# Pacing of a background chain: shorter pause in the inverse transform, Gram sums in one row, more table buffers

## The chip, the cores and the metric

The kernel runs on one core of a Trainium2 chip. The metric is the device time of one launch in microseconds, the median of several runs. Before the change it is 6687.31 us, the median of 3 runs from 6674.74 to 6688.99. The engines are TensorE (PE, matmuls), VectorE (DVE), ScalarE (ACT), GpSimd (POOL) and SyncE (SP), each with its own instruction queue that is worked in order. Lines such as L1301 are lines of the kernel before.

## The reference

The input x has 16 images of 32 channels of 128 x 128. Four layers follow one another, each adding its result to its input after a group normalisation `_gn`:

```python
x = x + _L0_conv_ref(_gn(x), ...)  # a recurrence over skewed columns, 128 steps
x = x + _L1_conv_ref(_gn(x), ...)  # 3x3 sums of |patch - weight|, 32 outputs, quantised
x = x + _L2_conv_ref(_gn(x), ...)  # Hartley transform, mix of 32 x 32 modes, transform back
x = x + _L3_conv_ref(_gn(x), ...)  # five edge operators, normed, conv1..conv7 with pooling and upsampling
```

Layer 3 needs, for each image, the mean and the standard deviation of the five edge pictures over all channels and pixels. The kernel gets these from Gram sums: products of neighbouring rows of the picture with themselves, multiplied with fixed tables and summed.

## The kernel before

**Three parts.** Layer 0 runs first (to about 670 us). Then layer 1 runs for the 16 images in turn, the main part, to 5587 us. Layers 2 and 3 run for four groups of four images each: groups 0 to 2 in the background of the main part, one after the other, each once its images are ready; group 3 at the end, together with what is left of group 2. This end is called the drain here.

**The main part** (class `Differences`). For each half image 72 difference tiles are made, one by one on DVE (L760, `d_dve`, 2.36 us) or on ACT (L757, `d_act`, 7.15 us). PE sums each of them into four PSUM banks (L647). Three buffers hold DVE's tiles and two hold ACT's. PE fills gaps with matmuls on zeros (L677, `keep_busy`).

**The order is planned while the program is written out.** Background work (class `After`) is a generator. It yields a positive number for PE work of so many microseconds, a negative one for a pause, or `SUMMED` for "until PE has finished". After each difference tile the main loop calls `Weave.advance`, which takes steps of the generator as long as planned time allows; a pause holds the background back until the planned time of DVE has passed it, so it is in effect rounded up to whole difference tiles. Then `keep_order` fixes the order on every engine. Planned times only set the order; on the chip each engine takes its next instruction as soon as its semaphores allow. `later(us, step)` puts off a step, mostly a DMA on SP, in the same way.

**The drain** (function `drain`) has two such generators, the rest of group 2 on four PSUM banks and all of group 3 on four others. The one whose planned time is less goes next, and pauses are stretched by 1.5. When one has ended, the other runs alone with all eight banks. Group 3 has a copy of the object with buffer counts of its own (`"t_r": 8, "gm": 5, "e_v": 6` among them), so the counts that the diff changes are those of groups 0 to 2.

**A group's chain** is: `forward` (transform, L1103 to L1231), `back` (back products L1278; then 16 iterations of column products L1323 and the take-outs), `statistics` (Gram matmuls L1428, then 20 table sums L1492), scaling of the folded weights (L1559, L1561), `conv1` (L1747, eight chunks of 25 taps), the small convolutions (L1597) and upsamplings (L905), and `last` (L1876).

**The take-out** (`take_out`, L1296) of iteration n adds two PSUM tiles to the residual `xr[n]` (L1301) and takes statistics of it (L1303). Some planned microseconds later the result is stored to DRAM (L1307) and, later again, the residual n + 4 is loaded into the same buffer (`reload`, L1257); both DMAs are on SP. There are four such buffers (`t_r`) for groups 0 to 2. The next iteration's products are issued right behind the take-out, into the PSUM tiles that the take-out before last has freed.

**The table sums** multiply each of four Gram tiles (one an image) with each of five tables `gm`. With three table buffers the fourth and fifth tables are loaded by POOL (L1500) when the first and second have been used. The folded weights `v` come in ten halves through a ring of `e_v` buffers, also loaded by POOL.

Of the kernel before, what the change touches and what calls it, by code (L numbers as in the profile page):

```python
# [350 lines left out]
class Weave:  # L351
# [10 lines left out]
    def __init__(self, work):  # L362
        self.work, self.pending = work, None
        self.pe = self.dve = self.act = self.now = self.base = 0.0
        self.until = self.ready = 0.0
        self.draining = self.alone = False
        self.stretch = 1.0
        self.finished, self.count, self.put_off, self.for_act, self.ends = -1, 0, [], [], {}
# [590 lines left out]
class After:  # L959


    def __init__(self, nc, tc, side, sm, ps, cst, bias, a, d, stat, out):
        self.nc, self.tc, self.side, self.ps, self.cst, self.bias = nc, tc, side, ps, cst, bias
        self.a, self.d, self.stat, self.out = a, d, stat, out
        self.spare, self.banks = None, 0
        self.sm, self.scales = sm, {}
        self.buffers = {"t_x": 4, "xm": 3, "xw": 2, "t_w": 3, "t_r": 4, "frames": 2, "gm": 3, "e_v": 3, "l_x": 2}
        store = [d["up"][i] for i in range(3)]
        self.up5 = Composed(nc, sm, a, "deconv1", "conv5", bias[:, 7:8], bias[:, 4:5], store[0])
        self.up6 = Composed(nc, sm, a, "deconv2", "conv6", bias[:, 8:9], bias[:, 5:6], store[1])  # L970
        self.up7 = Composed(nc, sm, a, "deconv3", "conv7", bias[:, 9:10], bias[:, 6:7], store[2])
# [269 lines left out]
    def back(self, g, load):  # L1241
# [6 lines left out]
        with self.pool("t_z") as zp_, self.pool("t_r", ahead) as rp:  # L1248
# [47 lines left out]
            def take_out(n, pf):  # L1296
                while ready.get(n):
                    weave.done(ready[n])
                for r in range(2):
                    v = xr[n][:, r]  # L1300
                    nc.vector.scalar_tensor_tensor(v, pf[r], 2.0**-15, v, ALU.mult, ALU.add)  # L1301
                for r in range(2):
                    nc.vector.bn_stats(stat[:, 2 * n + r, :], xr[n][:, r])  # L1303
                weave.dve += 2.8

                def store():
                    nc.sync.dma_start(rows(n)(x3), xr[n])  # L1307
                    ready[n + ahead] = weave.later(6.0, lambda: reload(n + ahead)) if n + ahead < 16 else None

                ready[n + ahead] = weave.later(4.0, store)  # L1310
# [6 lines left out]
            for n in range(16):  # L1317
                s, half = n // 2, n % 2
                pf = [self.acc() for _ in range(2)]
                for i in range(4):  # L1320
                    for r in range(2):
                        part = slice(64 * half + 32 * r, 64 * half + 32 * r + 32)
                        nc.tensor.matmul(  # L1323
                            pf[r][:, W * i : W * i + W],
                            o1[part, 4 * s + i].rearrange("p b o -> p (b o)"),
                            cst["cas_t"][part, :],
                            start=True,
                            stop=True,
                        )
                yield 0.8  # L1330
                if previous:
                    yield -3.2
                    take_out(*previous)
                previous = n, pf
            yield SUMMED
# [65 lines left out]
    def statistics(self, g, pool, frames, sides, out, tables):  # L1401
# [12 lines left out]
        gm = [pool.tile([128, GRAM], F32, name="gm", bufs=tables_ahead) for _ in range(tables_ahead)]  # L1414
# [74 lines left out]
        for k in range(5):  # L1489
            for blk in range(4):  # L1490
                w = pool.tile([128, GRAM], F32, name="es_w", bufs=1)
                nc.vector.tensor_tensor_reduce(  # L1492
                    w, gram[blk][:, :GRAM], gm[k], 1.0, 0.0, ALU.mult, ALU.add, accum_out=red[:, blk, k : k + 1]
                )
                weave.dve += 0.7
                if blk % 2:
                    yield -0.4
            if len(gm) < 5:
                gm.append(pool.tile([128, GRAM], F32, name="gm", bufs=tables_ahead))
                nc.gpsimd.dma_start(gm[-1], self.a["gram"][:, len(gm) - 1])  # L1500
# [554 lines left out]
```

## Time and profile before

The profiled execution took 6656.74 us, with a span of 6655.0 us from its first to its last instruction; the median of the timed runs is 6687.31 us.

| stretch | us | what runs |
|---|---|---|
| layer 0 | 0 to about 670 | recurrence |
| main part alone | 683 to 1838 | difference tiles only |
| group 0 | 1838 to 3383 | background beside difference tiles |
| group 1 | 3406 to 4946 | the same |
| group 2, first part | 4963 to 5587 | up to the scaled weights, before conv1 |
| drain | 5590 to 6655 | rest of group 2 and group 3; group 3 alone from about 6317 |

| in the span | PE | DVE | ACT | POOL |
|---|---|---|---|---|
| busy us | 5351.9 | 5541.6 | 5455.3 | 66.4 |
| share | 80% | 83% | 82% | 1% |

A profile line "A <- B: total, times, longest" is the time for which A's engine stood idle before A, and what ended the wait. In a timeline each row has start, duration, engine, line and operation, with the idle time before it in brackets. A matmul of float32 is two records in the trace, so 32 records are 16 matmuls of the program.

### The profile page before, as it was taken

Reading aid. Unit: us, or ns where it says so; the run is one execution under the profiler, and the core shown is the slowest. Engines: PE = TensorE matmul, PEld = TensorE weight load, DVE = VectorE, ACT = ScalarE, POOL = GpSimd, SP = SyncE. Lnnn points to the kernel's source line nnn. Section 1 sums busy time; section 2 is a strip of 40 time slices with the busy share of each in tenths; the row PEclk is TensorE's granted clock in tenths of the full one; section 3 lists DMA queues with packets and bytes.
Section 4 is the critical chain, followed back from the end, with each engine's and each line's share of the span. In section 5 each row is a group of like instructions: output and inputs, shape, how many; then the busy total and the mean of one; then the engine's idle time right before and its main releaser. Section 6 shows DMA issues by size and latency. Waiting matters only on the chain.

```text
span 6655.0 us, 270517 instructions
## 1 busy us (share of the span) xinstructions
PE 5351.9 (80%) x126760; PEld 2793.3 (42%) x126760; DVE 5541.6 (83%) x6848; ACT 5455.3 (82%) x3201; POOL 66.4 (1%) x67
## 2 busy tenths in 40 slices
PE   3698677787777879998877778999787787986896
PEld 3675333333343433333333443333333443444584
DVE  7898899999999889999999999999999996243222
ACT  3898899999999989999999999999999996111112
POOL 0000000000000000000000000000000000000000
PEclk9999899999989989998999899999989898997897
DMA  7553322211343632211553652231355354345314
GB/s 318 209 190 121 80 58 63 54 40 47 76 135 109 185 106 64 66 43 48 115 144 92 176 157 67 66 78 35 79 137 148 88 168 127 133 155 161 100 32 108
DMA packets 380773, 728.15 MB, mean 109 GB/s; under 512 B 73284, under 2 KB 225348, under 8 KB 368772
## 3 DMA queue, kind: packets, MB, share of 16 engines
q1 hardware_dynamic: 372180, 676.41, 35.4%
q0 software_dynamic: 7040, 33.80, 1.5%
q8 instruction: 992, 16.25, 1.0%
q14 instruction: 129, 1.06, 0.1%
q10 hardware_dynamic: 432, 0.64, 0.0%
HBM read 510.69 MB, written 200.00 MB: 107 GB/s over the span
## 4 chain that ended last, share of the span: by engine, by line
issue 33%; PE 29%; DVE 21%; ACT 13%; DMA 4%; SPq 1%; POOL 0%; DVEq 0%; ACTq 0%; POOLq 0%
DVE d_dve L760 12%; PE acc L1747 11%; ACT d_act L757 8%; PE acc L647 7%; PE pg L223 3%; PE acc L905 3%; ACT gt L237 2%; PE acc L1597 1%; DVE stat L124 1%; DVE y L1685 1%; ACT junk L198 1%; PE acc L1428 1%; DMA v<-fold_d 1%; DMA xm_d<-xm 1%; ACT th L247 1%
## 5 line engine op out<-in xcount | busy, mean ns | idle before, releaser
L757 ACT ACTIVATE d_act<-q,neg 128x8192 f16<-128x8192 f16 (+1 forms) x628 | 4443.9, 7150 | 117.1 <-PE acc L647 95.1
L760 DVE TENSOR_SCALAR d_dve<-q,qw 128x8192 f16<-128x8192 f16 (+1 forms) x1676 | 3865.2, 2362 | 165.1 <-PE acc L647 146.1
L647 PE MATMUL acc<-d_dve,sel 128*32 128x512 f16 x26816 | 1874.2, 403 | 491.2 <-DVE d_dve L760 392.6
L647 PEld LDWEIGHTS <-sel 128*32 128x32 f16 x36864 | 1010.6, 100 | 2118.9 <-issue 1461.4
L1747 PE MATMUL acc<-xp,wf 32*32 32x512 f32 x25600 | 1000.9, 610 | 26.0 <-issue 17.5
L647 PE MATMUL acc<-d_act,sel 128*32 128x512 f16 x10048 | 734.1, 414 | 292.4 <-ACT d_act L757 285.3
L1688 ACT ACTIVATE y<-pooled,b 32x128 f32<-32x128 f32 x464 | 185.5, 400 | 513.1 <-DVE pooled L1674 506.8
L1747 PEld LDWEIGHTS acc<-xp,wf 32*32 32x32 f32 x25600 | 422.7, 104 | 373.1 <-issue 292.5
L677 PE MATMUL acc<-q,zero 128*32 128x512 f16 x6268 | 449.3, 399 | 0.0
L905 PE MATMUL acc<-y,u_conv 32*32 32x256 f32 (+1 forms) x9728 | 339.0, 453 | 88.5 <-issue 66.8
L223 PE MATMUL pg<-h,wb 64*64 64x20 f32 (+15 forms) x8192 | 341.4, 305 | 58.8 <-DVE h L251 33.7
L237 ACT ACTIVATE gt<-pg,bias 128x20 f32<-128x20 f32 (+15 forms) x1024 | 332.3, 384 | 40.1 <-PE pg L223 38.1
L223 PEld LDWEIGHTS pg<-h,wb 64*64 64x64 f32 x8192 | 251.5, 151 | 134.2 <-DVE h L251 81.1
L1428 PE MATMUL acc<-xp 32*64 32x204 f32 (+3 forms) x8576 | 241.1, 343 | 42.0 <-issue 40.2
L677 PEld LDWEIGHTS <-zero 128*32 128x32 f16 x6268 | 189.1, 101 | 172.8 <-issue 36.4
L1876 DVE SCALAR_TENSOR_TENSOR xr<-acc,l_one,xr 128x512 f32<-128x512 f32 x128 | 87.1, 743 | 199.0 <-PE acc L905 131.3
L905 PEld LDWEIGHTS acc<-y,u_conv 32*32 32x32 f32 x9728 | 155.6, 109 | 207.2 <-issue 158.1
L1846 ACT ACTIVATE xr<-xr,l_ms 128x1024 f32<-128x1024 f32 x64 | 68.7, 1145 | 209.7 <-DVE xr L1876 199.6
L1428 PEld LDWEIGHTS acc<-xp 32*64 32x64 f32 (+1 forms) x8576 | 170.2, 134 | 123.2 <-issue 115.4
L1782 DVE TENSOR_TENSOR acc<-acc,cut 128x4 f32<-128x4 f32 x256 | 35.3, 165 | 219.3 <-PE acc L1747 217.0
L223 PE MATMUL pg<-xn,wb 64*64 64x2 f32 (+63 forms) x4096 | 184.0, 290 | 25.9 <-issue 17.0
L1597 PE MATMUL acc<-y,w_conv 32*32 32x512 f32 (+2 forms) x4608 | 161.4, 506 | 46.9 <-DMA w_conv<-in_conv_dram 21.3
(218 smaller groups left out, 3653.4 us busy)
## 6 DMA issues: line engine op xcount, KB each, us to landing
q<-q_d SPq DMA_DIRECT2D x128, 536.2 KB, 10.1
xp<-xn_d SPq DMA_DIRECT2D x64, 660.0 KB, 5.0
xp<-x_d SPq DMA_DIRECT2D x56, 640.0 KB, 5.5
xr<-xn_d SPq DMA_DIRECT2D x64, 528.0 KB, 11.7
x_in<-in_x_dram SPq DMA_DIRECT2D x16, 2048.0 KB, 14.7
xn<-in_xs_dram SPq DMA_DIRECT2D x64, 512.0 KB, 7.0
res<-in_x_dram SPq DMA_DIRECT2D x64, 512.0 KB, 8.8
x_d<-res SPq DMA_DIRECT2D x64, 512.0 KB, 4.9
```

What stands on the lines that cost most here:

```text
L223: nc.tensor.matmul(bank[c][q][64 * pair : 64 * pair + 64, :, :width], wb[half, 4 * kind + KIND[q]].rearrange("p b o -> p (b o)"), v[half], ...
L237: nc.scalar.activation(gt[:, q, :, :n], bank[c][q][:, :, :n], AF.Tanh if q == G else AF.Sigmoid, bias=bias[:, KIND[q] : KIND[q] + 1],)
L647: self.nc.tensor.matmul(acc[k][32 * j : 32 * j + 32, :], self.sel16[:, i // 9, :], d[:, row : row + 4, c : c + W], start=first, stop=last,)
L677: self.nc.tensor.matmul(acc[k][32 * j : 32 * j + 32, :], self.zero, q[:, :4, :W], start=False, stop=False)
L757: nc.scalar.activation(dst, src, AF.Relu, bias=self.neg[:, i : i + 1])
L760: nc.vector.tensor_scalar(dst, src, self.qw[:, i : i + 1], 0.0, ALU.subtract, ALU.max)
L905: nc.tensor.matmul(acc[blk][32 * j : 32 * j + 32, o : o + rows * n], t[part, 4 * par + tap, :], src[part, top : top + rows, left : left + ...
L1428: nc.tensor.matmul(gram[blk][j : j + width, at : at + n], xp[part, l, 2 + j : 2 + j + width], xp[part, rows, j : j + width + 4], start=sta ...
L1597: nc.tensor.matmul(acc[blk][32 * j : 32 * j + 32, : rows * n], wc[name][part, tap, :], src[part, at : at + rows, kw : kw + n], start=tap == 0,
L1688: nc.scalar.activation(d, s, AF.Identity, bias=bj)
L1747: nc.tensor.matmul(acc[blk][32 * j : 32 * j + 32, :], tap_of("all", tap)[rows], xp[rows, 4 * j + kh : 4 * j + kh + 4, kw : kw + W], start= ...
L1876: nc.vector.scalar_tensor_tensor(v, acc[blk].rearrange("p (b r w) -> p r w b", b=2, w=64), one[:, blk : blk + 1], v, ALU.add, ALU.mult,)
```

## The change

Three edits. In `After.__init__` the table buffers `gm` go from three to five and the buffers of folded weights `e_v` from three to four. In `back` the pause ahead of each take-out goes from 3.2 to 1.4 planned microseconds. In `statistics` the pause of 0.4 after every second table sum is gone. With five table buffers all five tables are loaded at the start of `statistics`, and the load at L1500 is not reached. The last two edits act in the drain too.

```diff
@@ After.__init__
-        self.buffers = {"t_x": 4, "xm": 3, "xw": 2, "t_w": 3, "t_r": 4, "frames": 2, "gm": 3, "e_v": 3, "l_x": 2}
+        self.buffers = {"t_x": 4, "xm": 3, "xw": 2, "t_w": 3, "t_r": 4, "frames": 2, "gm": 5, "e_v": 4, "l_x": 2}
@@ After.back
                 yield 0.8
                 if previous:
-                    yield -3.2
+                    yield -1.4
                     take_out(*previous)
                 previous = n, pf
@@ After.statistics
                 weave.dve += 0.7
-                if blk % 2:
-                    yield -0.4
             if len(gm) < 5:
```

## The prediction

> **What bounds the kernel now.** I read the page's slices first, then the busy time by stretch, then the waits, then single instructions.
>
> ```profile
> PE   3698677787777879998877778999787787986896
> DVE  7898899999999889999999999999999996243222
> ACT  3898899999999989999999999999999996111112
> ```
>
> There are two regimes. Up to slice 34 VectorE (DVE) and ScalarE (ACT) are full, producing the difference tiles of layer 1; then they go nearly idle and TensorE (PE) carries the end. The last difference tile ends at 5587 us. The busy times (length, PE, PE weight loads, DVE, ACT, POOL, PE clock, DMA share, GB/s):
>
> ```profile
> 683.00:1838.00 1155.00, 898.11 (x15882) 432.19 (x15885) 1134.72 (x878) 1128.46 (x176) 0.00 (x0) 0.94 0.23 57
> 2384.00:2440.00 56.00, 28.17 (x325) 11.39 (x321) 52.80 (x96) 56.00 (x9) 9.54 (x9) 0.73 0.32 103
> 4038.00:4591.00 553.00, 526.98 (x11716) 199.58 (x11716) 519.86 (x331) 540.16 (x190) 0.00 (x0) 0.98 0.22 58
> 5232.00:5347.00 115.00, 87.66 (x1272) 48.11 (x1268) 115.00 (x106) 113.50 (x18) 0.00 (x0) 0.87 0.52 153
> 5860.00:5955.00 95.00, 89.95 (x2166) 51.01 (x2145) 50.15 (x97) 16.08 (x41) 0.00 (x0) 0.93 0.59 184
> 5955.00:6130.00 175.00, 119.11 (x3824) 75.47 (x3812) 57.11 (x199) 38.70 (x66) 5.80 (x11) 0.82 0.60 180
> ```
>
> These are: layer 1 alone; Gram sums and table products; conv1 inside the main part; the take-outs of group 2; the take-outs of group 3 in the drain; group 3's Gram matmuls. The first has 599 tiles in 1155 us, 1.93 us a tile. The background never rests: group 1 begins (3406) when group 0 ends (3383), group 2 (4963) when group 1 ends (4946). So a microsecond saved in any group's chain of steps moves everything after it forward, and more of group 2 is done before the drain.
>
> The pause decides the pace in the drain. DVE around three take-outs of group 3:
>
> ```profile
> 5879.09 1.29 DVE L1301 SCALAR_TENSOR_TENSOR xr<-acc,xr 128x512 f32<-128x512 f32 x2 [4.09 <-PE acc L1323]
> 5880.30 1.28 DVE L1303 BATCH_NORM_STATS2 stat<-xr 128x6 f32<-128x512 f32 x2
> 5885.66 1.29 DVE L1301 SCALAR_TENSOR_TENSOR xr<-acc,xr 128x512 f32<-128x512 f32 x2 [4.09 <-PE acc L1323]
> ```
>
> One iteration is 6.57 us, of which DVE works 2.57 and waits 4.09 for products that stand on PE behind five taps of the other group's conv1. In the main part an iteration of the steady stretch is 6.94 us: two difference tiles (4.67) and 2.6 of take-out. The risk is SyncE's queue, here in group 2:
>
> ```profile
> SPq L1307 <- DVE xr L1301: 118.2, 10, 87.0
> SPq L1257 <- DMA x_d<-xr: 53.5, 11, 13.9
> ```
>
> A residual's reload waits on SP until the store of its buffer has landed, once 13.9 us, while q loads were under way.
>
> **What the Trainium skill says.** "Perfetto Trace Analysis", section Optimization Strategy: where the most-contended engine changes between regimes, interleaving the regimes can help. The trace agrees: in the first stretch PE is busy 898 of 1155 us, so PE work moved there has room. "DMA: Bandwidth & Descriptors", section Anatomy of one DMA: a semaphore wait is made by the issuing sequencer before dispatch; the SP waits above are that. Same page, section Issuing engines are not separate DMA queues: loads issued by POOL share the same 16 engines; no run here separates the two. "TensorE: Matmul & The Clock Gate", section What's actually happening: PE falls to half clock after an idle window of about 3.4 us. The trace agrees in direction: clock 0.73 in the table stretch above.
>
> **The change part by part.** I compared the instruction orders of the two builds; they say where each step stands, not how long it takes.
>
> *Pause -3.2 to -1.4.* Difference tiles issued between first and last take-out of a group: 41, 41, 43 before; 25, 23, 26 after. Nothing is removed; 16 to 18 tiles per group move behind the take-outs.
>
> *Gram sums without pauses.* Only 3, 3, 3 tiles stand between the 20 sums before, 0, 1, 1 after: the sums take about 16 us now, and 20 x (0.594 + 0.082) = 13.5 us of DVE is their floor. At most 3 tiles per group. ACT hides the block with its two buffers (2 x 7.15 us); without that cover 13.5 us of ACT would idle per group.
>
> *Five table buffers.* Six loads of 210 KB move from behind the sums (L1500) to the start of the stage, on POOL, whose 67 busy us are 1% of the span. Their landing (3.6 us median) is hidden by some 130 us of Gram matmuls; without cover it would cost 6 x 3.6 = 22 us. DVE's idle before the sums names only the Gram matmuls as releaser, so I take 0.
>
> *Four fold buffers.* DVE waited for these loads 8.1 us in the whole main part (8 times, longest 2.1). Worth 0 to 8; I take 0.
>
> Sum of the lead: where group 2's table scaling ends, the after-build is 81 tiles earlier. At the last difference tile it has 848 of conv1's 3200 matmuls behind it, where before it had none.
>
> *Main part.* DVE gains 8 poolings (0.688), 16 cut additions (0.165) and 4 copies (estimate 0.2), 8.9 us; its tiles change by +21 x 2.384 - 19 x 2.350 = +5.4: in all +14.3. ACT gains 16 evictions (0.400), 6.4, and its tiles change by +19 x 7.118 - 21 x 7.226 = -16.5: -10.1. Weighted by what each makes (one tile in 2.36 or 7.15 us, shares 0.75 and 0.25): **+8 us**. Cross-check: conv1 inside the main part runs 543 us with 269 tiles, 2.02 a tile, so 74 tiles more of it cost 74 x 0.09 = 7. PE takes the matmuls instead of 592 filler matmuls (L677).
>
> *Drain.* A conv1 tap is 16 matmuls in 1.16 us (32 records in 1.17 us in the timeline), 0.0725 each. Gone: 848 x 0.0725 = 61.5, and about 3.5 of edge matmuls: 65 us. By stage, from matmul counts of the two orders: up to group 3's first back product conv1 has 1936 before, 1952 after, no difference. In the take-outs the other group gives 800 matmuls before, 288 after; DVE becomes the limit there: 16 x 2.57 = 41, plus two rounds of conv2 evictions (8 x about 1.8 = 14), 55 us for 89 (5863 to 5952): -34. From there to group 3's conv1 400 small-conv matmuls less stand against 384 upsampling ones more: 0. After it 384 fewer upsampling matmuls (339 us for 4864, 0.07 each): -27. Together -61. Against it I set 14 us, estimates: 8 for the stores, because 16 stores and 8 reloads of 0.5 MB in 55 us are 229 GB/s where 184 took 0.59 of the DMA engines; and 6 for the unbroken block of sums, behind which the other group's evictions wait on DVE, up to 13.5. **-47 us**.
>
> Sum: 6656.7 - 47 + 8 = 6618 for the profiled execution, -39 us or -0.6%. The profiled execution was 30.6 below the median of the timed runs, so I put the same difference on the median: 6687 - 39 = **6648**.
>
> *What is late next.* The moved tiles lose nothing, but the four residual buffers now turn in four short iterations: 2.6 us of take-out plus some 1.1 tiles, 5.2 us. In the usual new order reload n+4 stands on SP behind store n+1. It lands at about 5.2 + 1 + 4.2 (the median landing) = 10.4 us after take-out n ends; take-out n+4 starts at 4 x 5.2 - 2.6 = 18.2. Slack 7.8 us. Behind that reload SP holds later stores and the q loads for both engines. Where q loads fall into the stage (groups 0 and 2), a store's landing of 14 us instead of 5 uses the slack up: 0 to 12 us in all, inside the range.
>
> **Rivals.** *A, nothing left (6683).* The drain is held by latencies, not PE work: its Gram stretch has PE busy 119 of 175 us, and the upsampling that moves into it waits on evictions. Then only a part of the take-out gain stays, say 12 of 34 after the stores' backlog, against +8: -4. For it: those gaps. Against: the other drain stretches have PE at 90% or more up to 5955.
>
> *B, slower (6729).* The reloads come late in every iteration of the main part. Place: L1301 waiting for the reload of L1257. Price: 36 reloads x 0.75 = 27 us for each microsecond of lateness. It decides once the trip passes 18.2 by 39 / 27 = 1.4 us; at 3 us late, +81 - 39 = +42. For it: the 13.9 us wait and DMA shares of 0.52 to 0.60. Against: reload landings of 3.4 to 4.7 us in that stage, and no DVE wait for a residual before.
>
> *C, all of it (6625).* No backlog, no hold-up by the sums: -61 or a little more, main part nearly free because ACT ends earlier: -62.
>
> *D, the sums and buffers do nothing*, only the pause acts. This is half in the forecast already: 3 tiles, 6 us a group at most.
>
> **How the numbers follow.** Forecast 0.60 (own range 6630 to 6673), A 0.13, B 0.11, C 0.16. A measurement of this kernel can tell about 0.2%, 13.4 us: faster means below 6674. Forecast and C are faster, 0.76; A is within, 0.13; B slower, 0.11. The range 6618 to 6688 leaves out B and part of C.
>
> **What would show it.** Right: take-outs of a main group in 80 to 90 us (103 to 115 now); L1747 records before the last difference tile; that tile at about 5595; group 3's take-outs in about 55 us with no 4 us waits; span near 6618. Wrong: DVE waits at L1301 for a DMA; difference tiles waiting for PE by much more than 146 us; the end of the main part beyond 5610; a longer gap between group 3's take-outs and its Gram matmuls (now 53 us).

## Result and the profile after

The changed kernel takes 6647.09 us (median of 4 runs, 6630.3 to 6654.34) against 6686.53 before (4 runs, 6674.74 to 6688.99): ratio 0.9952, 95% interval 0.9937 to 0.9968. Measured a second time, it took 6640.0 against 6666.88, ratio 0.9960 (0.9948 to 0.9972). So it is faster by 0.4 to 0.5%, 27 to 39 us. Profile against profile it gained 26.4 us, 6656.74 to 6630.3.

The slices of the page after show the same two regimes:

```profile
PE   3698677787777879997887879998877879887896
DVE  7898899999999989998999999999999998242322
ACT  3898899999999999998999989999999998102112
```

The last difference tile ends at 5604 us (5587 before); from there to the end it is 1025 us (1068 before). The main part cost some 15 us, the drain gave 43. Busy times after, with the prediction's columns: take-outs of group 2; conv1 of group 2 inside the main part, which was not there before; take-outs of group 3; group 3's Gram matmuls; the whole drain.

```profile
5126.00:5203.00 77.00, 57.42 (x732) 31.94 (x725) 74.19 (x85) 77.00 (x12) 0.00 (x0) 0.84 0.73 227
5459.00:5604.00 145.00, 136.95 (x3204) 55.65 (x3196) 140.36 (x88) 144.65 (x38) 0.00 (x0) 1.00 0.12 36
5887.00:5964.00 77.00, 60.05 (x1051) 38.88 (x1048) 58.09 (x135) 0.00 (x0) 0.00 (x0) 0.70 0.69 214
5993.00:6136.00 143.00, 100.19 (x3345) 61.26 (x3318) 25.36 (x68) 36.98 (x60) 0.00 (x0) 0.87 0.72 194
5604.00:6628.00 1024.00, 825.12 (x25757) 532.16 (x25746) 312.16 (x866) 177.51 (x339) 7.97 (x15) 0.86 0.43 120
```

The drain of the kernel before, for comparison:

```profile
5587.00:6655.00 1068.00, 874.92 (x27636) 561.26 (x27635) 318.01 (x886) 187.23 (x364) 7.94 (x15) 0.89 0.41 118
```

PE is busy 50 us less in the drain and idle 6 us more (193 to 199), which makes the 43 us less there. In the main part, DVE in the take-outs of group 1 after the change (timeline):

```profile
3653.53 1.29 DVE L1301 SCALAR_TENSOR_TENSOR xr<-acc,xr 128x512 f32<-128x512 f32 x2
3654.73 1.28 DVE L1303 BATCH_NORM_STATS2 stat<-xr 128x6 f32<-128x512 f32 x2
3655.92 2.34 DVE L760 TENSOR_SCALAR d_dve<-q,qw 128x8192 f16<-128x8192 f16 x1
3658.18 1.29 DVE L1301 SCALAR_TENSOR_TENSOR xr<-acc,xr 128x512 f32<-128x512 f32 x2
```

One tile stands for each take-out where there were two, 4.65 us an iteration where it was 6.94, and no idle time in brackets. PE in group 3's take-outs, first before the change, then after it (`...` stands for rows left out):

```profile
5877.90 1.16 PE L1323 MATMUL acc<-cw,o 32*128 32x128 f32 x16
5878.99 5.55 PE L1747 MATMUL acc<-xp,wf 32*32 32x512 f32 x160
```

```profile
5904.81 1.16 PE L1323 MATMUL acc<-cw,o 32*128 32x128 f32 x16
5905.90 3.41 PE L1595 MATMUL acc<-y,w_conv 32*32 32x512 f32 x96
...
5926.24 2.12 PE L1595 MATMUL acc<-y,w_conv 32*32 32x256 f32 x36 [10.85 <-DMA w_conv<-in_conv_dram]
...
5939.63 2.66 PE L1323 MATMUL acc<-cw,o 32*128 32x128 f32 x16
```

Where five taps of conv1 stood between two products, there are now up to three of conv2 or a part of one of conv3. The third row ends a wait of 10.85 us for the weights of conv3, which stood on SP's queue behind a reload. That wait is not new: before the change PE waited for the same weights in the stage behind the take-outs, and longer:

```profile
PE acc L1597 <- DMA w_conv<-in_conv_dram: 21.3, 1, 21.3
```

The last row is a product that takes 2.66 us where the first took 1.16.

### The profile page after: what moved, and what is told of

It is laid out like the page before. It is cut to its first block, busy times and chain, and to the rows that moved or that the text cites. A ratio compares the mean times of both kernels' runs of the same rounds, so it can differ in the third digit from the quotient of the medians.

```text
span 6628.4 us, 269240 instructions
## 1 busy us (share of the span) xinstructions
PE 5329.5 (80%) x126168; PEld 2776.6 (42%) x126168; DVE 5552.5 (84%) x6858; ACT 5436.8 (82%) x3191; POOL 69.9 (1%) x67
## 4 chain that ended last, share of the span: by engine, by line
PE 32%; issue 29%; DVE 20%; ACT 14%; DMA 3%; SPq 1%; POOL 0%; DVEq 0%; ACTq 0%; POOLq 0%
DVE d_dve L760 12%; PE acc L1745 11%; ACT d_act L757 10%; PE acc L647 9%; PE pg L223 3%; PE acc L905 3%; PE acc L1595 2%; PE acc L1428 2%; ACT gt L237 2%; DVE y L1683 1%; ACT junk L198 1%; DVE stat L124 1%; DMA x_in<-in_x_dram 1%; ACT th L247 1%; DVE pooled L1672 1%
## 5 line engine op out<-in xcount | busy, mean ns | idle before, releaser
L647 PE MATMUL acc<-d_dve,sel 128*32 128x512 f16 x26848 | 1873.4, 402 | 441.7 <-DVE d_dve L760 375.9
L647 PEld LDWEIGHTS <-sel 128*32 128x32 f16 x36864 | 1002.0, 100 | 2084.2 <-issue 1413.5
L1745 PE MATMUL acc<-xp,wf 32*32 32x512 f32 x25600 | 971.3, 607 | 19.0 <-issue 15.6
L647 PE MATMUL acc<-d_act,sel 128*32 128x512 f16 x10016 | 727.2, 412 | 311.5 <-ACT d_act L757 298.4
L677 PE MATMUL acc<-q,zero 128*32 128x512 f16 x5676 | 406.5, 398 | 0.8 <-issue 0.8
L677 PEld LDWEIGHTS <-zero 128*32 128x32 f16 x5676 | 169.4, 101 | 156.0 <-issue 30.5
L1780 DVE TENSOR_TENSOR acc<-acc,cut 128x4 f32<-128x4 f32 x256 | 36.3, 165 | 233.0 <-PE acc L1745 230.4
L1373 ACT ACTIVATE xp<-xp,shift,stats 128x1280 f32<-128x1280 f32 (+1 forms) x64 | 91.4, 1433 | 162.6 <-DVE shift L1341 111.6
```

What stands on the lines that cost most here:

```text
L647: self.nc.tensor.matmul(acc[k][32 * j : 32 * j + 32, :], self.sel16[:, i // 9, :], d[:, row : row + 4, c : c + W], start=first, stop=last,)
L677: self.nc.tensor.matmul(acc[k][32 * j : 32 * j + 32, :], self.zero, q[:, :4, :W], start=False, stop=False)
L1373: nc.scalar.activation(v, v, AF.Identity, bias=self.shift3, scale=self.stats3[:, 1])
L1745: nc.tensor.matmul(acc[blk][32 * j : 32 * j + 32, :], tap_of("all", tap)[rows], xp[rows, 4 * j + kh : 4 * j + kh + 4, kw : kw + W], start= ...
```

## Experiments

Ratios are to the kernel before on the same chip, measured beside each run anew (medians of 6666.88 to 6679.03 us). "Moved" counts the conv1 matmuls of group 2 that the order places before the last difference tile, of 3200; it is 800 for the whole change. The prediction's 848 counted to that tile's own sums on PE, a little later. The main part is from the first to the last difference tile and the drain from there to the end, in one profiled execution each.

| kernel | moved | main part us | drain us | PE busy in drain | ratio, interval |
|---|---|---|---|---|---|
| before | 0 | 4901 | 1068 | 875 | 1 |
| pause in the drain alone | 0 | 4907 | 1079 | 884 | 1.0003 (0.9995 to 1.0011) |
| sums and buffers alone | 257 | 4910 | 1054 | 853 | 0.9978 (0.9967 to 0.9989) |
| pause in the main part alone | 657 | 4918 | 1024 | 840 | 0.9939 (0.9925 to 0.9952) |
| pause alone | 657 | 4925 | 1026 | 837 | 0.9944 (0.9930 to 0.9957) |
| whole, sums with pauses | 657 | 4922 | 1024 | 835 | 0.9931 (0.9918 to 0.9943) |
| whole change | 800 | 4916 | 1025 | 825 | 0.9952 (0.9937 to 0.9968) |
| whole change, again | 800 | 4923 | 1030 | 831 | 0.9960 (0.9948 to 0.9972) |
| whole, old pause in the drain | 800 | 4923 | 1038 | 821 | 0.9961 (0.9948 to 0.9975) |
| whole, weights on POOL's queue | 800 | 4927 | 1028 | 833 | 0.9958 (0.9945 to 0.9971) |
| whole, three residual buffers | 800 | 4933 | 1040 | 836 | 0.9966 (0.9953 to 0.9979) |
| whole, group 1's sums later | 721 | 4916 | 1024 | 839 | 0.9945 (0.9933 to 0.9957) |
| more pauses cut | 913 | 4923 | 1022 | 816 | 0.9970 (0.9958 to 0.9982) |

Kernels with the same order in the main part differ by 6 us (4901, 4907) and by 11 (four with the whole change's order: 4916, 4923, 4923, 4927), so a few microseconds of one profile mean nothing. The intervals of most of the faster kernels overlap with one another too: what sets them apart is read from their traces below, and the medians alone don't show it.

### The pause in the main part alone

```diff
-                    yield -3.2
+                    yield -3.2 if weave.draining else -1.4
```

> The kernel before, with the shorter pause (1.4) only in the main part; the drain keeps 3.2, and sums and buffers stay as before. In its instruction order 657 of conv1's 3200 matmuls of group 2 stand before the last difference tile (848 with the whole change, none before). Theory 1, matmuls moved out of the drain are the gain: 657 x 0.0725 = 48 us less in the drain, less about 6 in the main part and about 10 lost to waits, so 30 to 38 us faster than before, ratio 0.994 to 0.996; last difference tile at about 5594. Theory 2, group 3's own chain of steps sets the drain and the shorter pause there is the gain: within 8 us of before, ratio 0.999 to 1.001.

6640.64 us against 6678.1: 37 us faster, as theory 1 had it and far from theory 2. The last difference tile ended at 5609, not at 5594. Busy times of its drain, to be held against those before (875 of 1068 us for PE):

```profile
5609.00:6633.00 1024.00, 840.02 (x26082) 530.07 (x26066) 316.92 (x886) 174.46 (x332) 7.95 (x15) 0.86 0.43 121
```

### The pause in the drain alone

```diff
-                    yield -3.2
+                    yield -1.4 if weave.draining else -3.2
```

> The kernel before, with the shorter pause only in the drain; the main part's order is as before. Theory 1: the same matmuls in another order, 0 to 10 us faster, ratio 0.9985 to 1.000; the take-outs of group 3 shorter than 89 us, and what they leave out done after them. Theory 2: 25 to 40 us faster, ratio 0.994 to 0.996.

6680.51 against 6678.1: no gain at all. Yet group 3's take-outs did shorten, from 88 us to 58 from first to last. Busy times of that stretch and of the drain in this kernel:

```profile
5877.00:5934.00 57.00, 55.29 (x1189) 29.68 (x1186) 40.63 (x74) 6.40 (x16) 0.00 (x0) 0.91 0.62 184
5596.00:6675.00 1079.00, 883.63 (x27664) 546.79 (x27648) 315.24 (x878) 190.56 (x372) 7.97 (x15) 0.89 0.41 117
```

PE was full in the shorter stretch too. Group 3 reached its conv1 22 us earlier (592 us into the drain, 614 before), and then that conv1 took 303 us in place of 272, because the other group's matmuls that had been left out came back beside it: that group ended at 761 us, not at 728. Theory 2 is out: where PE is full, letting one chain pass only reorders.

### The pause alone, in both places

```diff
-                    yield -3.2
+                    yield -1.4
```

> The kernel before with the shorter pause in both places, sums and buffers as before. Theory 1: the sum of the two runs above, 30 to 45 us faster, and so close to the whole change (39 us), since the sums and the buffers are worth little. A rival by which the sums or the buffers carry the gain: 10 to 20 us faster.

6643.23, 35 us faster: the pause accounts for the gain, and the shorter pause in the drain adds nothing to it.

### Sums and buffers alone

```diff
-        ... "gm": 3, "e_v": 3, "l_x": 2}
+        ... "gm": 5, "e_v": 4, "l_x": 2}
...
-                if blk % 2:
-                    yield -0.4
```

> Sums in one row and the buffer counts, with the old pause of 3.2. In its order 257 conv1 matmuls stand before the last difference tile: 257 x 0.0725 = 19 us less in the drain, and a few us lost in the main part to the unbroken block of sums. Theory 1: 8 to 16 us faster, ratio 0.9975 to 0.999. A rival by which the block of sums costs more than it gives: no faster, ratio 1.000 or more.

6661.87 against 6678.1: 16 us faster, at the upper end of theory 1. So this part alone has a worth too. But the 35 of the pause and these 16 don't add up to the 27 to 39 of the whole.

### The whole change without the pause in the drain

```diff
-                    yield -1.4
+                    yield -3.2 if weave.draining else -1.4
```

> The whole change, but with the old pause of 3.2 in the drain. The shorter pause alone in the drain gave nothing. Theory 1 (only matmuls moved into the main part count): the same as the whole change, 33 to 48 us faster than before. Rival: with less of the other group's work left in the drain the shorter pause there does count, and without it 10 us or more of the gain go: 15 to 30 us faster.

6654.16 against 6679.03, ratio 0.9961 (0.9948 to 0.9975), 25 us. The number falls in the rival's range, but the whole change itself gave 0.9960 when it was run again. In the profiles the drain is 1038 us against 1025 and 1030, and the take-outs 90 against 69. The other group ended 634 us into the drain here, about when group 3's conv1 began (631), so group 3's own chain was what lasted. The profiles lean to the rival, by some 10 us, but the medians don't show it: whether the shorter pause is worth that much there stays open.

### The whole change with the sums' pauses put back

```diff
                 weave.dve += 0.7
+                if blk % 2:
+                    yield -0.4
```

> The whole change, but with the pause of 0.4 after every second sum put back. Its order has 657 conv1 matmuls before the last difference tile, against 848. Theory: the 20 us for which ACT stood still at 3874 in the whole change came from the unbroken sums standing before the end of a half image, and is gone here; so the main part is 3 to 6 us shorter while the drain is 191 x 0.0725 = 14 us longer: 25 to 38 us faster than before, the same as the shorter pause alone (35), since buffers do nothing. Rival: the ACT gap has another cause and stays.

6634.56 against 6679.03, ratio 0.9931: 44 us faster, more than expected and more than the whole change. The drain was not 14 us longer though 143 matmuls fewer were moved: 1024. The long ACT stop is gone: the longest wait of ACT's tiles for PE is 8.0 us. The main part was not shorter (4922). From the end of group 1's conv1 to group 2's take-outs it took 118 us more than its tiles would at 1.93 us each, where it was 90 before and 87 in the whole change, and DVE's tiles waited there 43 us for PE's sums (L647), 17 before and 21 with the whole change. With the shorter pause in the main part alone and in both places it was 35 and 39 us, and the stretch cost 109 and 112. So the different order lost elsewhere what it won at the sums; which step held PE there was not followed further. This kernel has the lowest ratio of the study, but its interval overlaps with those of the pause alone; against the whole change it is clear in the second of that kernel's two measurements (0.9943 against 0.9948) and overlaps in the first.

The ACT stop that this was about, first in the waits of the main part, before and after the change (waiting < releaser: us in total, times, longest):

```profile
ACT d_act L757 <- PE acc L647: 95.1, 39, 9.3
```

```profile
ACT d_act L757 <- PE acc L647: 125.7, 48, 20.2
```

The longest wait in the timeline of the whole change, around group 1's table sums (rows picked out, the rest left out):

```profile
3852.48 21.24 ACT L757 ACTIVATE d_act<-q,neg 128x8192 f16<-128x8192 f16 x3
3879.21 0.59 DVE L1492 CUSTOM_DVE_ANT_0 es_w<-acc,gm 128x420 f32<-128x420 f32 x1
3888.70 2.72 DVE L628 SCALAR_TENSOR_TENSOR xr<-acc,sumw,xr 128x512 f32<-128x512 f32 x4
3889.50 2.59 PE L647 MATMUL acc<-d_dve,sel 128*32 128x512 f16 x16 [8.60 <-DVE xr L628]
3893.91 21.25 ACT L757 ACTIVATE d_act<-q,neg 128x8192 f16<-128x8192 f16 x3 [20.19 <-PE acc L647]
```

ACT ends a tile at 3873.7 and has both buffers full. They are freed by PE's sums (L647), which need the PSUM banks of the half image just ended. DVE has to take those out (L628), and in DVE's order this stands behind all 20 sums (from 3866.8 to 3879.8), a tile and the small steps after them. So ACT stands for 20.2 us. The sums fell onto the end of a half image: the 21st in the order has its last tile at 1512, the sums stand at 1514, and the take-out of the half image comes behind them.

### Group 1's sums four tiles later

```diff
-        yield -1.0
+        yield -9.0 if g == 1 else -1.0
```

> The whole change, with one pause of 9 ahead of group 1's table sums. They then stand 4 difference tiles later, behind the end of the half image instead of ahead of it, still in one row. Theory, the ACT stop of 20 us comes from the place of the block and not from its length: no such stop, the stretch from group 1's sums to its conv1 costs 24 us beyond its tiles and not 38, so the main part is some 13 us shorter for the same work. In the order 721 in place of 800 conv1 matmuls are ahead in the same count, so 5 us more in the drain: 5 to 10 us faster than the whole change. Rival, the length alone stops ACT: the 38 stay and the kernel is slower than the whole change by about 5.

6631.92 against 6666.88, ratio 0.9945 (0.9933 to 0.9957), where the whole change had 0.9960 on the same chip: 8 us less, as the theory said, though the intervals overlap. ACT's waits in that stretch:

```profile
ACT d_act L757 <- PE acc L647: 4.4, 2, 3.8
```

The block is as long as before and ACT no longer stops. From group 1's first sum to the first edge product of its conv1 (L1719) it is 47 us with 12.3 tiles, 24 us beyond 1.93 us a tile; in the whole change 60 us with 11.1 tiles, 38 beyond, and 38 or 39 in the four other profiles with that order. With sums and buffers alone, whose block stands at tile 1556, it is 24 too. It was the place and not the length. How much of these 14 us the main part keeps is not clear: it took 4916 us, where the whole change took 4916 and 4923.

### The weights of conv3 and conv4 on POOL's queue

```diff
-                wc[n] = replicated(nc, cp, self.a[n], 9, f"w_{n}")
+                wc[n] = replicated(nc, cp, self.a[n], 9, f"w_{n}", nc.gpsimd)
```

> The whole change, with the weights of conv3 and conv4 loaded on POOL's queue, not on SP's. Theory: the 10.9 us for which PE waited for these weights in the middle of group 3's take-outs came from SP, where the loads stood behind a reload that waited for a store; without it the take-outs of group 3 take some 10 us less, and the kernel is 5 to 11 us faster than the whole change, 44 to 50 faster than before. Rival: PE's total is what counts and it catches up elsewhere, so no difference from the whole change, 39.

6651.24 against 6679.03, ratio 0.9958 (0.9945 to 0.9971): no gain over the whole change. PE's wait for those weights, whole change first, then this kernel:

```profile
PE acc L1595 <- DMA w_conv<-in_conv_dram: 10.8, 1, 10.8
```

```profile
PE acc L1595 <- DMA w_conv<-in_conv_dram: 1.2, 1, 1.2
```

The wait is gone and the take-outs take 62 us in place of 69. But group 3's conv1 begins 600 us into the drain (601), and the drain takes 1028 us (1025). The cause was right and the gain was not there.

### Three residual buffers

```diff
-        ... "t_r": 4, "frames": 2, "gm": 5 ...
+        ... "t_r": 3, "frames": 2, "gm": 5 ...
```

> The whole change with three residual buffers in place of four for groups 0 to 2; the order of the difference tiles and of conv1 in the main part is the same. An iteration measured 4.65 us, a reload's way (store, its landing, load) about 10.2 after the take-out. With four buffers the next use comes 16.1 us after, with three 11.4: about 1 us of slack, none where q loads or other stores are under way. Theory of the slack: DVE waits for reloads in all three groups, 1 to 3 us each time, 20 to 60 us in all, times 0.75: the kernel is 10 to 45 us slower than the whole change, so between 30 faster and 10 slower than before. Rival: reloads are far from late, and nothing changes (39 faster).

6659.45 against 6679.03, ratio 0.9966 (0.9953 to 0.9979): 20 us faster than before, 4 to 9 us behind the whole change by the medians' ratios. DVE's waits from 1838 us to the end of the main part:

```profile
DVE xr L1301 <- issue: 10.5, 2, 5.9
```

Two waits, one each in groups 0 and 2, where q loads fall into the stage, and none in group 1. The view names nothing that ended them; that they are late reloads is argued from the buffer count. So the estimate of about 1 us of slack with three buffers was too small, and the price is under the low end expected. With four buffers the whole change shows a single wait for a DMA at this line, 1.8 us.

### More pauses cut

```diff
-            if ky % 4 == 3 and 8 < ky < M1 - 1 and not weave.draining:
-                yield -2.5
...
-                yield -1.2
+                yield -0.4
```

The sums' pauses are put back here.

> The whole change with the pauses between the sums put back, and two more pauses of the main part's background cut: 2.5 in the mixing left out, 1.2 between the scalings of the folded weights to 0.4. 913 conv1 matmuls are ahead in the same count (657 with the sums' pauses back alone, 800 with the whole change). Theory 1 without a limit: 256 x 0.055 = 14 us faster than the run with the sums' pauses back, so about 60 faster than before. Rival, a limit: the drain does not get shorter than about 1025 us, since group 3's own chain holds it there once the other group has little left, and the gain stays at 35 to 48.

6643.79 against 6666.88, ratio 0.9970: 23 us faster, less than the whole change. The drain took 1022 us:

```profile
5611.00:6633.00 1022.00, 815.97 (x25586) 528.91 (x25574) 312.17 (x867) 171.54 (x324) 7.95 (x15) 0.86 0.43 120
```

PE's work fell again, from 825 to 816 us, but its idle time rose to 206. From 657 moved matmuls to 913 the drain went from 1024 to 1022. The rival is right on the drain: beyond some 650 there is nothing more to gain there. The gain itself, 23 us, is under the rival's 35 to 48 too; in the profile the main part, 4923 us, is no longer than with 657 moved (4918 to 4925), so the rest of it is not accounted for. In addition ACT stopped for 18.0 us ahead of group 1's conv1.

### The whole change again

> The whole change once more, as it is, so that the runs of this call are compared with it on the same chip: 32 to 42 us faster than before.

6640.0 against 6666.88: 27 us, less than expected. Its main part, 4923 us, is 7 longer than in the first profile, and the ACT stop of 20.2 us is there again.

## Why the prediction was right, and where it was not

The forecast of 6648, 39 us faster, was met (6647.09); measured again the gain was 27 us, so the nearness of the first figure is luck. The mechanism is shown: the shorter pause in the main part is enough for the whole gain, the one in the drain gives none, and the drain gets shorter by about as much as PE has less to do there. Its parts were met less well.

| step | predicted | measured, profile to profile |
|---|---|---|
| main part | +8 | +15; +18 as the mean of four executions against two |
| drain up to group 3's take-outs | 0 | +14 (277 to 291) |
| group 3's take-outs | -34 | -19 (88 to 69) |
| take-outs to group 3's conv1 | 0 | -8 (249 to 241) |
| from there to the end | -27 | -31 (455 to 424) |
| set against it, unplaced | +14 | in the rows above |
| sum | -39 | -29; -27 with layer 0, which took 2 longer |

**Signs named ahead.** conv1 did come ahead of the last tile, and DVE's tiles waited for PE hardly more than before (149 us against 146). But the last tile came at 5604 and not at about 5595, the take-outs of groups 0 to 2 took 69 to 77 us and not 80 to 90, and group 3's still had waits of up to 5.2 us.

**Main part.** The step "ACT hides the block with its two buffers" failed in group 1, and the prediction's own price without that cover, 13.5 us, is what the stretch cost (38 us beyond its tiles, 24.6 before). That is not all of it: the kernels without this stop have a main part that is no shorter (4916 to 4925), because they lost in another stretch. So the +8, which weighed the evictions and tiles that moved, was too small in every order with the shorter pause: it left out what a new order makes DVE and ACT wait for.

**Drain up to the take-outs.** The matmul counts were equal, as said, but the whole change has one new wait of PE there, whole change, after the last difference tile:

```profile
PE acc L1214 <- DVE acc L1780: 15.0, 1, 15.0
```

In the timeline (rows picked out):

```profile
5722.82 0.17 DVE L1186 COPY xw<-xs 64x32 f32<-64x32 f32 x1 [17.78 <-DMA xw<-xm_d]
5731.60 0.17 DVE L1186 COPY xw<-xs 64x32 f32<-64x32 f32 x1 [5.31 <-DMA xw<-xm_d]
5733.55 1.16 DVE L1193 SCALAR_TENSOR_TENSOR xs<-xw,cw,xs 64x465 f32<-64x465 f32 x4
5734.74 0.44 DVE L1780 TENSOR_TENSOR acc<-acc,cut 128x4 f32<-128x4 f32 x4
5734.92 1.89 PE L1214 MATMUL acc<-xs,mix 128*32 128x8 f32 x124 [15.04 <-DVE acc L1780]
```

At 5720 PE had ended a chunk of the other group's conv1, and next in its order stood group 3's mixing (L1214). It reads `xs`, which the flips of the modes (L1193) write, and these waited on DVE for their loads (17.8 and 5.3 us); the last flip ended at 5734.7. The view names conv1's evictions (L1780), which stood on DVE behind the same flips; the mixing does not read what they write, and they only happened to run last. So PE stood on group 3's loads, with conv1's next chunk behind the mixing. The wait is 14.5 to 14.8 us in the four other profiles with this order. With 657 matmuls moved DVE waited for these loads as long (33 us in all, 30 here), but PE shows no such wait. Counting matmuls did not see that.

**Readings of the lines.** The 53 us that the prediction names for the gap between group 3's take-outs and its Gram matmuls ran to 6005, behind the wait of 21.3 us for conv3's weights; the first Gram matmuls came 26 us after the take-outs. The parts of an iteration (4.67 and 2.6 for 6.94 us) add up to too much because consecutive DVE rows overlap by about 0.1 us.

**Take-outs.** "DVE becomes the limit there, 55 us" did not hold. The run with the pause in the drain alone comes near the number (58 us), but for another reason: PE was full there (55.3 of 57 us), and DVE waited 17.3 us for it. In the whole change DVE worked 51 of 69 us. PE, with less to do, waited 10.8 us for weights, and a product then took up to 3.1 us, so that DVE waited for PE again, 17.3 us here too. Of the 14 us set against the sum, the part for a backlog of stores did come, in another form: just ahead of the issue of these weights SP waited twice for a store so that it could issue a reload, 11.0 us in all. The part for the sums does not show (PE waited 2.5 us for them at group 3's sums, 5.8 before), and the 14 was not meant for the wait at the mixing or for slow products. It covered them all the same; that the sum came out near is partly luck.

**Take-outs to conv1.** The 0 forecast became -8. Group 3's Gram stage no longer holds the wait of 21.3 us for the weights; a wait of 10.8 us for them lies in the take-outs instead.

**Sums and buffers.** Alone they give 16 us with 257 matmuls moved, about what "3 tiles, 6 us a group at most" makes for three groups. What failed is adding their lead to that of the pause. Together with the pause they give nothing measured, because the drain's gain had ended at some 650 moved matmuls, and because their place cost ACT its stop. This limit is what the prediction lacked: it priced all 848 at 0.0725 us each, 61.5 us, where PE's busy time fell by 50 and the drain by 43. The traces narrow down where the limit lies. From the end of group 3's conv1 to the end of the kernel it is 183 to 188 us in every run, before the change too, and in that conv1 PE is busy 236 of 239 us. PE's idle time is ahead of it, 115 of 614 us before, 135 of 601 with the whole change and 137 of 600 with more pauses cut. Which step of group 3's chain holds it there was not isolated.

**Rival B** (late reloads) is out: one wait of 1.8 us with four buffers, 10.5 us with three. **Rival A** fits in its mechanism, gaps of group 3's chain that no work fills, but as a limit and not in place of the gain. **Rival C** is out by its own terms: the main part was not nearly free, and the stores did hold up the weights. **Rival D** holds for the sum, since beside the pause the sums and buffers add nothing measured; but alone they do act. Of the two, the buffers show nothing: the whole change with the sums' pauses put back differs from the pause alone in the buffers only, has as many matmuls moved, and its interval overlaps.

## What to carry to other kernels

Work moved from a tail into a stage with room is worth its time only until the tail is held by something else: test it with more and with less of the move, and stop where the tail no longer shortens. A pause in a hand-planned order pays or costs by what fills it; where the bound engine is full anyway, shortening it only reorders. And a block of work without breaks on an in-order queue has to be placed by what is queued behind it: the same 13 us of sums cost 14 us less four tiles later.

## What the runs showed of the hardware

**TensorE's clock in group 3's take-outs.** In the whole change sixteen product records (L1323) took 1.16 us ahead of the wait of 10.85 us and 2.66 us behind it, a factor of 2.3. In stretches of 4 us the granted clock was 1.00 from 5904 to 5916, fell to 0.74 and then 0.50 during the wait, and was 0.50 in each stretch from 5920 to 5952. "TensorE: Matmul & The Clock Gate", section What's actually happening, of the Trainium skill says that an idle window of about 3.4 us halves the clock, and the fall in the wait agrees. What this trace adds is that the clock then stayed low for 26 us while PE was busy on record:

```profile
5926.00:5952.00 26.00, 25.76 (x324) 18.52 (x326) 14.98 (x24) 0.00 (x0) 0.00 (x0) 0.50 0.81 249
```

In the run with the weights on POOL's queue the wait was only 1.2 us, and products still took 2.66 us (clock 0.69 over the take-outs). Over all runs the clock in this stage was 0.91 to 0.94 in the three kernels with up to 257 matmuls moved, where conv1 stood between the products for all or a part of the stage, and 0.65 to 0.75 in the ten with 657 or more. So there less work on PE went with slower products; that the one caused the other is argued and not isolated.
